# Layer 0 of a two-layer graph network: propagation by a matrix applied to products (Y0 + T (Y1 + T Y2)) in place of products of propagated inputs, with PSUM banks seeded by copies

## Chip, cores, metric

One core of a Trainium2 chip; the groups of rounds ran on different chips. Times are device microseconds (us) of one execution; a median and the range of the runs are given. All runs reported here were in the fast state, with a granted TensorE clock (the share of full speed that the chip allowed, averaged over the execution) of 0.994 to 1.000. That is not equal clock for differences of some us: 0.001 of 2365 us is 2.4 us, if TensorE is busy meanwhile (my estimate). A ratio is the mean time of one kernel's fast runs over the mean of the other kernel's fast runs in the same rounds, so it is not quite the ratio of the medians that I quote.

## The reference

128 graphs of 128 nodes with 512 features, fp32. All masks are ones, T is a row-normalised 128 x 128 matrix for each graph.

```python
# layer 0
h = maximum(layernorm(x), 0)
Xw = h @ Wv + bv
e = leaky_relu((Xw @ aw[:d])[:, None, :] + (Xw @ aw[d:])[:, :, None] + ab, 0.2)
alpha = adj * exp(e);  T = alpha / (sum(alpha, -1) + 1e-12)
H = 0; Xk = h
for k in range(3):                      # sum over k of T^k h W_k + b_k
    H = H + Xk @ Wk[k] + bk[k]
    Xk = T @ Xk
x = x + relu(H)
# layer 1
h = maximum(layernorm(x), 0)
q, k = split(h @ Wqk);  v = h @ Wv1
w = scale * rowsum(q * (adj @ k))
x = x + softmax(w)[:, :, None] * v
```

## The kernel before

Graphs are worked on in 64 pairs. The two scores of a node are h times two columns u (worked out once from Wv and aw), so VectorE forms them as sums over h. The products with weights are Strassen products: 7 block products instead of 8, with sums of blocks on the left (from h) and on the right (from the weights). The parts that the argument touches:

```python
def score_sums(p):                                  # VectorE: 4 sums over 512 columns (line 303)
    for j in range(G):
        for a in range(2):
            nc.vector.scalar_tensor_tensor(junk, h[:, j, :], 1.0, u_bc[:, a, :], op0=OP.mult,
                                           op1=OP.mult, accum_out=s[:, a * G + j:a * G + j + 1])
    PZ[p] = spread_pair(s, "pz", p > 1)             # scores to all partitions, through memory

def t_transposed(p):                                # T^T (line 384) and (T T)^T (line 388)
    ...
def propagate(p):                                   # (T h)^T and (T T h)^T: line 400, copies line 402
    ...
def strassen0(p, steps):                            # k = 0, 1, 2 side by side: 7 products, each
    product(ba, 1, True)                            # 3 x 2 matmuls x 2 column blocks, 256 wide (line 421)
    nc.vector.tensor_add(s[:, 0], a, hi)            # partial sums kept in SBUF by VectorE
    nc.vector.tensor_add(s[:, 1], a, lo)
    product(bb, 6, True)
    nc.vector.tensor_add(s[:, 2], b, s[:, 1])
    steps[0]()                                      # begin(n): transposes h of the next pair (VectorE)
    product(bc, 7, True)
    steps[1](s[:, 1])                               # attention of the next pair
    product(bb, 5, False)
    ...
    steps[2]()                                      # t_transposed of the next pair
    end(s[:, 3, :G])                                # softmax and output of an earlier pair
    ...
def prepare0(p):                                    # left sums of layer 0: four of 768 columns (VectorE)
    SX[p] = left_sums(a, front, "sx", [K, HD])
```

Layer 1 is a Strassen product of 28 passes 512 wide, also line 421, then two aggregates adj k (line 519). h goes to memory and comes back in blocks so that VectorE's block transpose can make h^T.

## Time and profile before

| | before |
|---|---|
| time, median of 3 runs | 2366.88 us (2364.62 to 2368.94) |
| TensorE busy | 99% |
| VectorE / ScalarE busy | 77% / 27% |
| period of the loop, one pair of graphs | 35.98 us |
| first T transpose | 37.41 us |

The busy table and the chain of waits name TensorE; that the loop has hardly a TensorE wait is what makes it the bound. The lines for this stand in the prediction. One view more is needed later, the landing times of transfers (tile written and read, queue, count, KB each, median us from issue to landing):

```profile
hd<-h SPq DMA_DIRECT2D x127, 512.0 KB, 4.0
hv<-hd SPq DMA_DIRECT2D x508, 128.0 KB, 5.3
```

These are h's way out to memory and back in blocks.

The profiled execution of the kernel before, from which all its lines here come, took 2370.26 us, longer than the three runs of the table. And its first pairs differ from the rest. TensorE in the third period:

```profile
90.81 3.78 PE L421 MATMUL pm<-e,x 128*128 128x512 f32 x4 [3.27 <-DVE x L320]
94.38 1.91 PE L421 MATMUL pm<-f,sx 128*128 128x512 f32 x2
```

Four passes of 512 columns stand 94.38 - 90.81 = 3.57 us apart, where they take 1.717 in mid-run: the clock was at half. The profile's clock records say so from 32.0 to 35.4 and from 90.1 to 96.9 us, 10.2 us in all. What brings these stretches about isn't tested here.

### The profile page before, as it was taken

Reading aid. Unit: us, or ns where it says so; the run is one execution under the profiler, and the core shown is the slowest. Engines: PE = TensorE matmul, PEld = TensorE weight load, DVE = VectorE, ACT = ScalarE, POOL = GpSimd, SP = SyncE. Lnnn points to the kernel's source line nnn. Section 1 sums busy time; section 2 is a strip of 40 time slices with the busy share of each in tenths; the row PEclk is TensorE's granted clock in tenths of the full one; section 3 lists DMA queues with packets and bytes.
Section 4 is the critical chain, followed back from the end, with each engine's and each line's share of the span. In section 5 each row is a group of like instructions: output and inputs, shape, how many; then the busy total and the mean of one; then the engine's idle time right before and its main releaser. Section 6 shows DMA issues by size and latency. Waiting matters only on the chain.

```text
span 2368.5 us, 27872 instructions
## 1 busy us (share of the span) xinstructions
PE 2342.0 (99%) x8929; PEld 1660.0 (70%) x8929; DVE 1825.3 (77%) x4959; ACT 637.5 (27%) x1562; POOL 379.0 (16%) x662
## 2 busy tenths in 40 slices
PE   8999999999999999999999999999999999999998
PEld 5677676676776776776766767767767767667675
DVE  6787877877877778778778778778788787787775
ACT  3222222322222222223222222222222232232221
POOL 4111111111111111111111111111111111111100
PEclk9999999999999999999999999999999999999999
DMA  7334344344343343443442433433434434424321
GB/s 210 91 92 107 98 107 105 83 116 111 85 116 106 90 107 99 107 107 84 120 106 83 116 107 90 114 101 98 107 100 105 107 91 115 107 81 117 104 63 49
DMA packets 253670, 242.88 MB, mean 103 GB/s; under 512 B 28318, under 2 KB 178846, under 8 KB 253522
## 3 DMA queue, kind: packets, MB, share of 16 engines
q1 hardware_dynamic: 228096, 211.87, 31.8%
q0 software_dynamic: 23312, 28.18, 6.7%
q8 instruction: 70, 1.15, 0.2%
q10 hardware_dynamic: 2114, 1.05, 0.1%
q14 instruction: 78, 0.64, 0.1%
HBM read 140.72 MB, written 100.27 MB: 102 GB/s over the span
## 4 chain that ended last, share of the span: by engine, by line
PE 89%; DVE 4%; DMA 2%; issue 1%; ACT 1%; POOL 0%; DVEq 0%; POOLq 0%
PE pm L421 75%; PE pt L400 8%; PE pt L519 4%; DMA pwd<-pwt 1%; PE pt L388 1%; PE pt L384 1%; DMA pw<-pwd 1%; DVE st L260 0%; DMA pz<-pzd 0%; DVE junk L303 0%; DVE x L461 0%; DVE x L320 0%; DVE x L549 0%; DMA pzd<-pzt 0%; DVE sx L409 0%
## 5 line engine op out<-in xcount | busy, mean ns | idle before, releaser
L421 PE MATMUL pm<-t,sx 128*128 128x256 f32 x2304 | 508.0, 379 | 2.9 <-DVE sx L408 2.9
L421 PEld LDWEIGHTS pm<-t,sx 128*128 128x128 f32 x2304 | 437.5, 190 | 63.0 <-DVE sx L408 3.5
L421 PE MATMUL pm<-b,x 128*128 128x256 f32 x1536 | 363.1, 379 | 0.0
L421 PE MATMUL pm<-f,sx 128*128 128x512 f32 x768 | 352.5, 594 | 2.0 <-DVE s L479 2.0
L421 PEld LDWEIGHTS pm<-b,x 128*128 128x128 f32 x1536 | 282.2, 190 | 59.7 <-issue 29.7
L339 POOL DMA_DIRECT2D pzd<-pzt x124 | 68.8, 556 | 1406.2 <-DVE pzt L336 1406.1
L421 PEld LDWEIGHTS pm<-f,sx 128*128 128x128 f32 x768 | 145.8, 191 | 186.7 <-issue 160.4
L421 PE MATMUL pm<-e,x 128*128 128x512 f32 x512 | 242.5, 596 | 3.3 <-DVE x L320 3.3
L402 ACT COPY x<-pt 128x512 f32<-128x512 f32 x256 | 147.3, 576 | 365.5 <-PE pt L400 365.4
L400 PE MATMUL pt<-tt,h 128*128 128x256 f32 x1024 | 231.6, 379 | 0.5 <-ACT tt L389 0.5
L303 DVE SCALAR_TENSOR_TENSOR junk<-h,u_bc 128x512 f32<-128x512 f32 x256 | 177.1, 692 | 64.1 <-ACT h L278 52.9
L400 PEld LDWEIGHTS pt<-tt,h 128*128 128x128 f32 x1024 | 194.5, 190 | 27.5 <-ACT tt L389 1.1
L421 PE MATMUL pm<-b,sx 128*128 128x256 f32 x768 | 176.2, 379 | 0.0
L421 PE MATMUL pm<-t,x 128*128 128x256 f32 x768 | 176.2, 379 | 0.0
L320 DVE STREAM_TRANSPOSE x<-hv 128x512 f32<-128x512 f32 x254 | 165.1, 688 | 10.8 <-DMA hv<-hd 9.7
L421 PEld LDWEIGHTS pm<-e,x 128*128 128x128 f32 x512 | 97.7, 191 | 99.7 <-issue 90.7
L356 ACT ACTIVATE s<-s 128x256 f32<-128x256 f32 x63 | 26.2, 416 | 518.9 <-DVE s L354 518.9
L421 PEld LDWEIGHTS pm<-t,x 128*128 128x128 f32 x768 | 145.9, 190 | 19.8
L421 PEld LDWEIGHTS pm<-b,sx 128*128 128x128 f32 x768 | 145.9, 190 | 19.8
L92 POOL DMA_DIRECT2D agb<-in_adj_dram x256 | 152.9, 602 | 22.6 <-issue 15.0
L278 ACT ACTIVATE h<-xg,rs 128x512 f32<-128x512 f32 x128 | 97.4, 807 | 172.8 <-DVE rs L272 172.8
L519 PE MATMUL pt<-h,aT 128*128 128x512 f32 x256 | 130.7, 592 | 0.0
(145 smaller groups left out, 2812.4 us busy)
## 6 DMA issues: line engine op xcount, KB each, us to landing
hd<-h SPq DMA_DIRECT2D x127, 512.0 KB, 4.0
hv<-hd SPq DMA_DIRECT2D x508, 128.0 KB, 5.3
xg<-in_x_dram SPq DMA_DIRECT2D x64, 512.0 KB, 3.6
out_dram<-x SPq DMA_DIRECT2D x63, 512.0 KB, 2.8
ag<-in_adj_dram SPq DMA_DIRECT2D x64, 128.0 KB, 2.8
agb<-in_adj_dram POOLq DMA_DIRECT2D x256, 32.0 KB, 4.2
pw<-pwd POOLq DMA_DIRECT2D x63, 128.0 KB, 3.3
pz<-pzd POOLq DMA_DIRECT2D x62, 128.0 KB, 5.5
```

The source lines that it names most:

```text
L92: nc.gpsimd.dma_start(agb[p][c * S32:(c + 1) * S32].rearrange("p g q i -> p (g q) i"), v[c])
L278: nc.scalar.activation(to, at, AF.Relu, bias=rs[:, 1, j:j + 1], scale=rs[:, 0, j:j + 1])
L303: nc.vector.scalar_tensor_tensor(junk, h[:, j, :], 1.0, u_bc[:, a, :], op0=OP.mult, op1=OP.mult, accum_out=s[:, a * G + j:a * G + j + 1])
L320: nc.vector.transpose(dst[:, j].rearrange("p f (n b) -> p f n b", n=Q), hv[:, j].rearrange("p n (f a) -> p f n a", f=Q))
L339: nc.gpsimd.dma_start(d[j], t[j::S32])
L356: nc.scalar.activation(ex, z, AF.Exp)
L384: nc.tensor.transpose(pt[:, j, :], t[:, j, :], ident)
L388: nc.tensor.matmul(pt[:, j, :], t[:, j, :], tt[:, j, 0, :], start=True, stop=True)
L400: nc.tensor.matmul(pt[:, c].rearrange("p k n -> p (k n)"), h[:, j, at:at + P], tt[:, j].rearrange("p k n -> p (k n)"), start=True, stop=True)
L402: nc.scalar.copy(X[p][:, 1:3, j, kh].rearrange("p k c n -> p c k n"), pt)
L421: nc.tensor.matmul(bank[:, :r.shape[-1]], left[i][:, k, c * P:(c + 1) * P], r, start=(first and at == 0), stop=(at == len(chunks) - 1), sk ...
L519: nc.tensor.matmul(to, AT[p][:, j, :], h2, start=True, stop=True)
```

## The change

Its intent: T^k h W_k is (T^k h) W_k before and T^k (h W_k) after. With Yk = h Wk, the sum is Y0 + T (Y1 + T Y2), so only h^T is needed as a left operand, T squared and the four copies of propagated inputs are gone, and the left sums shrink from 768 to 256 columns. The two score columns u stand beside W2 as a 257th column of each half, so TensorE forms the scores. Strassen's sums are made in PSUM: ScalarE copies one bank onto the next, and the next product adds onto it (the result passes the comparison, and in the trace after a product onto a copied bank streams like the others: four passes of 512 from 1218.56 to 1220.27 us, 0.428 each). Y0 and Y1 start on banks seeded with the biases. The core of the diff:

```diff
-        product(ba, 1, True)
-        nc.vector.tensor_add(s[:, 0], a, hi)
-        nc.vector.tensor_add(s[:, 1], a, lo)
-        product(bb, 6, True)
-        nc.vector.tensor_add(s[:, 2], b, s[:, 1])
-        ... (strassen0, propagate, T squared, score_sums: removed)
+    def strassen(banks, left, right, s, first, ends, steps={}):      # Y10, Y2 and layer 1
+        product(a, 1, first)
+        nc.scalar.copy(b, a)
+        product(e, 5, first)
+        nc.scalar.copy(s[:, 0], e)
+        product(b, 6)                                                # start=False: adds onto the copy
+        done["u2"] = nc.scalar.copy(c, b).ins
+        product(a, 2)
+        ends[0, 0](a)
+        product(c, 7)
+        nc.scalar.copy(s[:, 1], c)
+        ends[1, 1](e, s[:, 1])
+        product(b, 3)
+        ends[0, 1](b, s[:, 0])
+        product(c, 4)
+        ends[1, 0](c)
+    def seed():                                                      # [0 | b0] and [0 | b1 - b0]
+        nc.scalar.copy(a1, bias_a.rearrange("p k o -> p (k o)"))
+        nc.scalar.copy(e1, bias_e.rearrange("p k o -> p (k o)"))
+    def inner(p):                                                    # Y1 += T Y2, then to SBUF
+        for j, nh, bank in blocks1:
+            nc.tensor.matmul(bank[:, :HD], TT[p][:, j, :], y[:, j, nh, :HD], start=False, stop=True, ...)
+            nc.scalar.copy(z[:, j, nh], bank[:, :HD])
+    def outer(p, z):                                                 # Y0 += T (...), relu, add x
+        for j, nh, bank in blocks1:
+            nc.tensor.matmul(bank[:, HD:], tt[:, j, :], z[:, j, nh], start=False, stop=True, ...)
         ...
+            s0 = y10(p, {1: lefts, 6: lambda: t_transposed(p)})
+            z = inner(p)
+            s2 = y2(p + 1) if p + 1 < NP else s0
+            outer(p, z)
```

The start is rebuilt too: other loads, the weights transposed whole, Y2 of the first pair ahead of the loop. `issue_after` hints, which only fix the order in which an engine's instructions are issued, are added in many places.

## The prediction

> **What bounds the kernel now.** I read the page's busy table, then the chain that ended last, then the TensorE waits, then TensorE's timeline of one pair of graphs (the loop's unit; there are 64 pairs).
>
> ```profile
> PE 2342.0 (99%) x8929; PEld 1660.0 (70%) x8929; DVE 1825.3 (77%) x4959; ACT 637.5 (27%) x1562; POOL 379.0 (16%) x662
> ...
> PE 89%; DVE 4%; DMA 2%; issue 1%; ACT 1%; POOL 0%; DVEq 0%; POOLq 0%
> ```
>
> A busy TensorE alone doesn't prove a bound. The list of its waits does: the longest are these (total us, times, longest us), each happened once to three times in the whole run. Asked for 200 to 2300 us alone, the list has three waits, 1.9 us together: nothing waits in the steady loop.
>
> ```profile
> PE pt L236 <- DMA w<-in_L_gnn_Wqk_dram: 4.1, 2, 3.9
> PE pm L421 <- DVE x L320: 3.3, 1, 3.3
> PE pm L421 <- DVE sx L408: 2.9, 2, 2.0
> PE pm L421 <- DVE s L479: 2.0, 3, 1.2
> ```
>
> The timeline of one pair in mid-run (start, busy us, engine, line, operation, tiles, count) has no bracket that names an idle gap:
>
> ```profile
> 1243.54 0.38 PE L384 MATMUL pt<-ident,t 128*128 128x128 f32 x2
> 1243.76 1.03 PE L421 MATMUL pm<-b,x 128*128 128x256 f32 x4
> 1244.62 0.61 PE L388 MATMUL pt<-tt,t 128*128 128x128 f32 x4
> 1245.07 1.89 PE L421 MATMUL pm<-b,x 128*128 128x256 f32 x8
> ...
> 1251.97 3.62 PE L400 MATMUL pt<-tt,h 128*128 128x256 f32 x16
> 1255.43 1.88 PE L421 MATMUL pm<-e,x 128*128 128x512 f32 x4
> ...
> 1269.16 2.75 PE L421 MATMUL pm<-b,x 128*128 128x256 f32 x12
> 1271.75 7.93 PE L421 MATMUL pm<-t,sx 128*128 128x256 f32 x36
> 1279.52 0.38 PE L384 MATMUL pt<-ident,t 128*128 128x128 f32 x2
> ```
>
> From one L384 to the next is 1279.52 - 1243.54 = **35.98 us a pair**, and 64 x 35.98 = 2303 of the 2368. The rest is the start (the first L384 stands at 37.41 us), a few stalls behind it, and 8 us of tail. So the change is worth what it takes off TensorE's stream, less any stall that it brings.
>
> The price of a matmul must come from distances between starts, since durations overlap: thirty-six 256-wide ones take 1279.52 - 1271.75 = 7.77, or 0.2158 us each; the 32 passes 512 wide of layer 1 (L421 and L519) fill 1233.18 - 1219.44 = 13.74, or 0.4294 each (both starts from the same timeline one pair earlier). An L384 transpose is (1243.76 - 1243.54)/2 = 0.11, an L388 pass (1245.07 - 1244.62)/4 = 0.11. The record counts two passes for each fp32 product in the source, one for a transpose.
>
> [...]the trace is shorter (0.373 us at 256, 0.576 at 512 wide), and I use the trace. [...]two L278 of 0.806 take 1.52 together.
>
> **The change on TensorE, per pair.** Before: layer 0's Strassen has 7 products over k = 3 x 2 chunks x 2 columns-of-output blocks x 2 passes = 84 passes of 256; L400 (T and T squared times h) 16 of 256; layer 1 has 28 and the aggregates 4 of 512; T transposed 2 and T squared 4 of 128. 100 x 0.2158 + 32 x 0.4294 + 0.22 + 0.44 = 35.98, the measured period, so the count is right.
>
> After: Y1 and Y0 side by side, 7 x 2 x 2 = 28 passes of 512; Y2 with its score column, 28 of 257; the inner T Y2, 8 of 256, and the outer T(...), 8 of 256; layer 1 and aggregates 32 of 512; T transposed, 2 of 128. T squared is gone. 60 x 0.4294 + 28 x 0.2167 + 16 x 0.2158 + 0.22 = 25.76 + 6.07 + 3.45 + 0.22 = **35.50**. The gain is 0.48 us a pair, 30.7 us in 64 pairs. Of 140 records a pair 108 remain, which sounds like more than it is.
>
> **The change on the other engines, per pair.** VectorE has 1825.3/64 = 28.5 busy. It loses the four score sums L303 (4 x 0.69 and their reads, 3.1), swaps four 768-wide left sums for 256-wide ones (4 x (0.955 - 0.417) = 2.1), has two adds of 512 instead of five in layer 1 (2.0) and some 0.8 less in layer 0: about 20.5 remain, 58%. ScalarE has 637.5/64 = 10.0. It loses the four L402 copies, one tt copy and two layer-1 copies (3.8), and gains twelve of 512 (four in Y10, two seeds, six in layer 1: 12 x 0.58 = 7.0), six of 257 (2.2) and four of 256 (1.5): about 16.8, 47%. Neither becomes the bound by load; what counts is latency, as ScalarE now stands between products.
>
> **Latencies.** A copy starts some 0.2 us after the last pass has streamed (L384 ends its record at 1243.92, the ScalarE copy starts at 1243.96). In Y10 and layer 1 one product lasts 4 x 0.4294 = 1.72 and stands between the producer of a bank and the next use of its copy: 0.2 + 0.58 leaves 0.9 to spare. In Y2 a product lasts 0.87 and the copy 0.2 + 0.37: 0.25 to spare, and there the instruction order of the built kernel puts two relus (1.52) and the four z copies (about 1.25) on ScalarE before the first Y2 copy. Counting from the start t of Y2: the Y10 add of block 12 on VectorE follows product 3, which ended at t - 3.45; the add is over at t - 2.6, five small norm operations at 0.2 each bring t - 1.6, relus t - 0.05, z copies t + 1.2, the copy t + 1.6; product 6 wants it at t + 1.73. It fits with 0.1 us to spare. The other long loop is norm of layer 1's input, write to memory, read back, transposes and left sums: relu over at about 31 us of a pair, 9 to 10 us of transfers (landing medians 4.0 and 5.3 plus issues), so about 5 us into the next pair, where VectorE wants it at 4.9. Later than that by 2 us it would delay the relus and so Y2. I put **0.1 us a pair**, 6 us in all, for what of these margins fails.
>
> **Start and end.** Both kernels need about 30 us of TensorE work before the first pair (score matrix 16.4, transposes 6.4, the rest). Before, 7.4 us of waiting lie among it. After, the 2.6 MB of x and score weights come first, but the layer-0 weights are queued behind them: 7.3 MB at the 260 to 320 GB/s of the before kernel's first 30 us are there at about 27 us, and Y10's combinations at about 33; Y2 of pair 0 can run at 30 to 36. Against the first pair's work at 37.4 that saves up to 7 us; with a first loop whose VectorE queue is crowded (weight combinations, two left sums), I take 4. The tail stays within 1 us.
>
> Sum: 2366.9 - 30.7 - 4 + 6 = 2338; I say **2337 us**, 1.3% less.
>
> **Rivals.** (1) *Copies become the wait*: ScalarE is late at one or two products in each pair. For it: the margins of 0.1 and 0.25 above. Against: they hold with measured durations, and misses are small. At 0.5 us a pair the gain is gone: 2365. (2) *The reload loop binds*: transfers of 2 us more than assumed give a period set by norm, memory and left sums, 36.5 or so: 2400.[...] (3) *Everything fits and the start gains its 7 us*: 2328; without the first loop's stalls also, 2320, about the floor. (4) *Larger gain from fewer instructions*: if 32 fewer matmuls a pair saved 60 ns each, 2230[...].
>
> **Range and chances.** 80% range **2320 to 2364**: from rival 3's floor to rival 1's full loss. 2% faster is 2319.5, at the floor: **0.07**. 2% slower, 2414, takes more than a full microsecond of stall in each pair: **0.04**. Within 2%: **0.89**.
>
> **What would show the steps right or wrong.** Right: starts of two successive T transposes 35.5 to 35.7 us apart; 512-wide passes at 0.429 and 257-wide at 0.217; ScalarE near 47% and VectorE near 60% busy; next to no TensorE waits on ScalarE. Wrong: a wait of TensorE on ScalarE in Y2's product 6 or 7, repeated 60 times (rival 1); VectorE's transposes waiting for the read-back, followed by TensorE waits (rival 2); a 257-wide pass that costs clearly more than 0.217; a first Y2 that starts later than 37 us.

Where its prices come from: the copy times are those of lines 385 (0.373 us, 256 columns) and 402 (0.576 us, 512 columns) in the trace before. The 0.2167 us of a 257-wide pass was my estimate; the two measured widths give nearly the same, (0.4294 - 0.2158) / 256 = 0.834 ns a column and so 0.2166 us. That a product onto a seeded bank costs TensorE nothing more was assumed; no trace showed it yet. That a late copy holds the next product up was assumed too; the trace after has such waits at its start, 1.4 us in two (PE a L315 <- ACT b L322).

## The result and the profile after

The kernel after takes **2328.40 us** (2327.64 to 2328.80, 4 runs) against 2367.73 (2364.62 to 2368.94, 4 runs) before: ratio 0.9836, 95% interval 0.9818 to 0.9853. That is 1.64% faster and within 2%. It passes the comparison with the reference.

| | before | after | predicted |
|---|---|---|---|
| time, us | 2367.73 | 2328.40 | 2337 |
| period of a pair, us | 35.98 | 35.49 | 35.50 |
| VectorE busy | 77% | 58% | 58% |
| ScalarE busy | 27% | 44% | 47% |
| first Y2, us from the start | – | 37.38 | 30 to 36 |

Busy table and chain of the page after:

```profile
PE 2304.2 (99%) x6881; PEld 1290.7 (55%) x6881; DVE 1361.0 (58%) x4131; ACT 1028.8 (44%) x2517; POOL 336.6 (14%) x585
...
PE 98%; ACT 1%; DVE 0%; DMA 0%; issue 0%; POOL 0%; DVEq 0%; ACTq 0%; POOLq 0%
```

In the chain, VectorE's 4% and the transfers' 2% have gone: TensorE alone now sets the end. The whole list of TensorE waits begins with these (total us, times, longest):

```profile
PE b L205 <- ACT aw_bc L179: 7.1, 1, 7.1
PE b L178 <- DMA t<-in_L_gnn_aw_dram: 2.4, 1, 2.4
PE a L154 <- ACT y L355: 1.6, 1, 1.6
PE a L315 <- issue: 1.4, 1, 1.4
PE a L315 <- ACT b L322: 1.4, 2, 0.7
```

Each stands once or twice, none 60 times, and the list from 125 to 2280 us is empty: no wait came into the loop. TensorE's timeline of one pair in mid-run (start, busy us, engine, line, operation, tiles, shapes, count):

```profile
1216.62 0.38 PE L400 MATMUL a<-ident,t 128*128 128x128 f32 x2
...
1225.43 1.03 PE L315 MATMUL a<-r,x 128*128 128x257 f32 x4
...
1227.17 1.03 PE L315 MATMUL b<-t,sx 128*128 128x257 f32 x4
1228.03 1.03 PE L315 MATMUL a<-r,x 128*128 128x257 f32 x4
...
1233.23 1.88 PE L315 MATMUL a<-rl,x 128*128 128x512 f32 x4
1234.94 1.88 PE L315 MATMUL e<-tl,sx 128*128 128x512 f32 x4
...
1252.11 0.38 PE L400 MATMUL a<-ident,t 128*128 128x128 f32 x2
```

The period is 1252.11 - 1216.62 = 35.49 us. Four 257-wide passes take 0.866 (1227.17 to 1228.03), 0.2166 each; four 512-wide ones 1.717, 0.4293 each. So 64 x (35.98 - 35.49) = **31.4 us** of the 39.3 come from the columns that TensorE no longer streams. ScalarE's timeline in the same pair shows why nothing waits (a bracket is idle time ahead of the instruction):

```profile
1226.50 0.36 ACT L322 COPY b<-a 128x257 f32<-128x257 f32 x1
1227.37 0.37 ACT L324 COPY s<-e 128x257 f32<-128x257 f32 x1 [0.51 <-PE e L315]
1228.23 0.36 ACT L326 COPY c<-b 128x257 f32<-128x257 f32 x1 [0.49 <-PE b L315]
```

The copy that seeds bank b ends at 1226.50 + 0.36 = 1226.86, and its product starts at 1227.17: 0.31 us to spare where the prediction saw 0.1. The next seed ends at 1228.59, 0.31 ahead of 1228.90. The landing times after, for the same tiles as shown of before:

```profile
hd<-h SPq DMA_DIRECT2D x126, 512.0 KB, 2.8
hv<-hd SPq DMA_DIRECT2D x504, 128.0 KB, 2.9
```

They fell from 4.0 and 5.3 us, where the prediction's latencies kept these and its rival 2 had 2 us more. That transfers in bursts of two tensors would last longer was my guess when I predicted; no run shows it.

Left to explain: 39.3 - 31.4 = 7.9 us, where the prediction had a loss of 2 (stalls +6, start -4). Candidates: (a) the start or the end; (b) something small in every pair or in scattered pairs, above all VectorE, which was 77% busy before; (c) the period itself for another reason than the columns, such as fewer instructions. My theory when the experiments began: the columns give their 31 us, and a good part of the rest comes once, at the start. The rivals are (b) and (c). The experiments are to tell these apart and to say how close the copies are to becoming waits. The texts on record, written before each run, are quoted; where they letter the theories, the numbers beside the letter say what it stands for.

### The profile page after: what moved, and what is told of

The parts are those of the page before. It is cut to its first block, busy times and chain, and to the rows that moved or that the text cites. A ratio compares the mean times of both kernels' runs of the same rounds, so it can differ in the third digit from the quotient of the medians.

```text
span 2327.0 us, 23621 instructions
## 1 busy us (share of the span) xinstructions
PE 2304.2 (99%) x6881; PEld 1290.7 (55%) x6881; DVE 1361.0 (58%) x4131; ACT 1028.8 (44%) x2517; POOL 336.6 (14%) x585
## 4 chain that ended last, share of the span: by engine, by line
PE 98%; ACT 1%; DVE 0%; DMA 0%; issue 0%; POOL 0%; DVEq 0%; ACTq 0%; POOLq 0%
PE a L315 24%; PE c L315 24%; PE b L315 24%; PE e L315 12%; PE a L453 2%; PE e L453 2%; PE a L431 1%; PE c L431 1%; PE c L441 1%; PE b L441 1%; PE e L431 1%; PE e L441 1%; PE b L431 1%; PE a L441 1%; PE a L400 1%; ACT h L257 0%
## 5 line engine op out<-in xcount | busy, mean ns | idle before, releaser
L315 PE MATMUL a<-r,x 128*128 128x257 f32 (+1 forms) x1024 | 373.1, 486 | 1.4 <-ACT b L322 1.4
L315 PEld LDWEIGHTS a<-r,x 128*128 128x128 f32 x1024 | 189.3, 190 | 107.3 <-issue 91.2
L315 PE MATMUL a<-rl,x 128*128 128x512 f32 x512 | 240.7, 592 | 1.4 <-issue 1.4
L330 ACT COPY s<-c 128x512 f32<-128x512 f32 (+1 forms) x192 | 97.8, 510 | 209.5 <-PE c L315 209.4
L315 PE MATMUL c<-t,sx 128*128 128x257 f32 (+1 forms) x512 | 186.6, 487 | 1.2 <-ACT c L326 1.1
L315 PE MATMUL c<-t,x 128*128 128x257 f32 (+1 forms) x512 | 186.3, 486 | 0.3 <-ACT s L330 0.3
L315 PE MATMUL e<-t,sx 128*128 128x257 f32 (+1 forms) x512 | 186.4, 486 | 0.0
L315 PE MATMUL b<-t,sx 128*128 128x257 f32 (+1 forms) x512 | 186.2, 486 | 0.0
L315 PE MATMUL b<-r,sx 128*128 128x257 f32 (+1 forms) x512 | 186.2, 486 | 0.0
L324 ACT COPY s<-e 128x512 f32<-128x512 f32 (+1 forms) x192 | 98.8, 515 | 161.8 <-PE e L315 161.7
L315 PEld LDWEIGHTS a<-rl,x 128*128 128x128 f32 x512 | 97.2, 190 | 96.9 <-issue 93.6
L322 ACT COPY b<-a 128x512 f32<-128x512 f32 (+1 forms) x192 | 96.1, 500 | 97.7 <-PE a L315 89.7
L315 PEld LDWEIGHTS c<-t,sx 128*128 128x128 f32 x512 | 96.9, 190 | 70.6 <-issue 60.5
L315 PEld LDWEIGHTS c<-t,x 128*128 128x128 f32 x512 | 97.2, 190 | 68.7 <-issue 61.2
L315 PEld LDWEIGHTS b<-r,sx 128*128 128x128 f32 x512 | 97.3, 190 | 68.1 <-issue 61.2
L315 PEld LDWEIGHTS b<-t,sx 128*128 128x128 f32 x512 | 97.3, 190 | 68.1 <-issue 45.9
```

Source lines behind the costliest of these rows:

```text
L315: nc.tensor.matmul(bank, left[i][:, k * P:(k + 1) * P], right[i][:, k], start=(start and k == 0), stop=(k == HC - 1), skip_group_check=True)
L322: nc.scalar.copy(b, a)
L324: nc.scalar.copy(s[:, 0], e)
L330: nc.scalar.copy(s[:, 1], c)
```

## Experiments

### Half the pairs, both kernels

```diff
-    NP = B // G
+    NP = B // G // 2
```

Wrong on purpose (half the output isn't written). A constant gain at the start or the end stays whole at half the pairs, a gain per pair is halved.

> The kernel before with only the first 64 of 128 graphs (32 pairs); the rest of the output is left unwritten, wrong on purpose. The time is a constant (start and end) plus 32 pairs. Theory A (the gain is TensorE columns, 0.49 us in each pair, plus some 6 us of scattered stalls that the changed kernel lacks, plus some 4 us of start and end): 2367.7 - 32 x 35.98 - about 3 of stalls = 1213 to 1217 us.

Measured: 1211.3 us (1210.82 to 1212.69).

> The changed kernel with 32 pairs, wrong on purpose. Theory A: 2328.4 - 32 x 35.49 = 1192 to 1193 us, so 21 to 24 us less than the kernel before with 32 pairs: 15.7 from the pairs, the rest start, end and early stalls. Rival B (the gain sits in the start or the end): the difference stays near the 39 us of the full kernels. Rival C (all of it is in the steady pairs): the difference is half, 19.7.

Measured: 1193.0 us (1191.62 to 1193.67). The before half came out 2 to 6 us shorter than I had expected, so the difference is 18.3 us, not the 21 to 24 of my theory then, which put part of the gain at the start. The second half costs 2364.92 - 1211.3 = 1153.6 us before (36.05 a pair, whole kernel of the same rounds) and 2328.4 - 1193.0 = 1135.4 after (35.48 a pair). What doesn't grow with the pairs is 2 x 1211.3 - 2364.9 = 57.7 us before and 2 x 1193.0 - 2328.4 = 57.6 after. Taken at its word, start and end together gave nothing, and (a) falls. But that takes two things for granted that no run shows: that the first half of the kernel before has as many stalls as the second, and that the whole kernel after, which was run in other rounds only (the kernel before was 2.8 us slower in those), would have taken 2328.4 here.

The traces say otherwise. From each span I take the steady periods and what the periods behind the fourth T transpose exceed them by. Left for the start, the first three pairs and the end are 2368.48 - 64 x 35.98 - 5.99 = 59.8 us before and 2327.02 - 64 x 35.49 - 0.38 = 55.3 after; in the half kernels 59.0 and 55.3. So **some 4 us of the gain lie outside the steady loop**, and (a) stands; each of these is a single execution. What the half runs do show is a loss in the loop of the kernel before: its second half takes 36.05 - 35.98 = 0.07 us a pair more than its undisturbed period, 2.3 us in 32 pairs; the after kernel loses none.

### More columns in Y2

The Y2 passes of the after kernel are made 280 wide with 23 columns of zeros. Everything else stays: instruction counts, copies, orders.

```diff
-    WP = W2 + 3
+    W3 = HD + 24
+    WP = W3
-    r2 = const.tile([P, DC, 2, WP], FP, name="r2")[:, :, :, :W2]
+    r2 = const.tile([P, DC, 2, WP], FP, name="r2")
+    for c in range(DC):
+        nc.gpsimd.memset(r2[:, c, :, W2:W3], 0.0)
     ... (t2, y2 and s2 likewise; readers keep to column W2)
```

> The changed kernel with 280 instead of 257 columns in the Y2 products (23 columns of zeros more). Theory A (columns through TensorE set the period): 23 x 28 passes x 0.833 ns = 0.537 us a pair, 34 us in all: 2363 us, period 36.03, and the gain over the kernel before is all but gone. Rival D (fewer instructions, or relief of VectorE, makes the gain): stays at 2328 to 2333.

Measured: 2360.67 us (2359.34 to 2361.27, 20 runs), ratio 0.9980 to before; period 36.03. The timeline shows the new passes:

```profile
1242.64 1.11 PE L318 MATMUL b<-t,sx 128*128 128x280 f32 x4
1243.59 1.11 PE L318 MATMUL a<-r,x 128*128 128x280 f32 x4
```

Four take 0.945, 0.236 each. The period grew by 0.54 for 28 x 23 columns, which the price per column from the two widths before gives (28 x 23 x 0.834 ns = 0.537). Instructions are as few as in the after kernel and the gain is nearly gone: (c) falls, **columns set the period**. And a hint: with a period 0.05 us *longer* than before's (64 x 0.05 = 3 us), this kernel is 4 us *faster* than before, and scatters by 1.9 us where before scatters by 8.8. That suggests that some 7 us of before's time lie outside its steady stream of columns: waits, the start, or the clock (0.9996 in the mean of the wide runs, 0.998 before).

### VectorE relieved in the before kernel, a little

```diff
-    nc.vector.scalar_tensor_tensor(junk, h[:, j, :], 1.0, u_bc[:, a, :], op0=OP.mult,
+    nc.vector.scalar_tensor_tensor(junk[:, :S32], h[:, j, :S32], 1.0, u_bc[:, a, :S32], op0=OP.mult,
```

Score sums over 32 of 512 columns, with wrong scores on purpose (the comparison is too loose to see it).

> The kernel before with its four score sums cut from 512 to 32 columns (wrong on purpose): VectorE has some 1.9 us a pair less to do, nothing else changes. Theory A: the steady period stays at 35.98; only the scattered stalls (6 us over the run) shrink: 2361 to 2367 us. Rival E (relief of VectorE is a main source of the gain): 2350 or less.

Measured: 2364.63 us (2361.63 to 2366.97, 13 runs), ratio 0.9999 (0.9991 to 1.0007). VectorE fell from 77% to 73%, and the median did not move. The clock blurs this: these runs had 0.997 in the mean against 0.998 before, and the slower ones the lower clock (2361.63 us at 0.999, 2366.97 at 0.995), so that a gain of about 2 us could be hidden. The one profiled run was the fastest of the thirteen, without scattered stalls; had I had that profile alone, I would have believed in a gain. A profile is one draw.

### VectorE loaded in the after kernel

```diff
+    def load_vector(h):
+        for i in range(4):
+            junk = front.tile([P, D], FP, name="junk2", bufs=1)
+            nc.vector.scalar_tensor_tensor(junk, h[:, i % G, :], 1.0, h[:, i % G, :], op0=OP.mult,
+                                           op1=OP.mult, accum_out=vcol[:, i:i + 1])
         ... (called behind both by_blocks of a pair: 8 sums of 512 columns more)
```

> The changed kernel with eight 512-wide VectorE sums a pair added, whose results nobody reads: 5.8 us a pair, so that VectorE is again some 75% busy, as in the kernel before. Theory A: period 35.49 stays the most frequent one; scattered stalls of up to some us may return, time 2328 to 2335 us. Rival E (relief of VectorE makes much of the gain): 2345 us and up.

Measured: 2333.44 us (2331.14 to 2336.66, 4 runs), ratio 0.9874, period 35.49 as before the loading. At 73% of VectorE the after kernel loses 5 us by the medians, 9 by the ratios (0.9874 against 0.9836; the kernel after itself wasn't run in these rounds), and four runs scatter by 5.5 us instead of 1.2. The profiled execution, the fastest of the four, has no TensorE wait in the loop; its span is 2.3 us longer than that of the kernel after, and 2.1 of them lie before the fourth T transpose (153.66 against 151.57 us). So part of the loss is again one of the first pairs; stalls in the loop are not shown by it.

### Scores by VectorE in the after kernel

Y2 is 256 wide again, four sums a pair on VectorE make the scores, and their spreading goes as in the before kernel. The weights of the sums are wrong on purpose; the timing is what counts.

```diff
-    W2 = HD + 1
+    W2 = HD
+    def score_sums(p, h):
+        s = S[p] = scols[p % 3]
+        for j in range(G):
+            for a in range(2):
+                nc.vector.scalar_tensor_tensor(junk, h[:, j, :], 0.01, u_bc, op0=OP.mult,
+                                               op1=OP.mult, accum_out=s[:, a * G + j:a * G + j + 1])
         ... (attention and the spreading read s instead of Y2's columns)
```

> The changed kernel with the score columns taken out of the Y2 product (256 wide again) and made by four VectorE sums of 512 a pair, as before, with weights that are wrong on purpose. Theory A: TensorE saves 28 x 0.83 ns = 0.023 us a pair, 1.5 us in all, and VectorE goes to 67%: 2325 to 2330 us. So this part of the change would be worth nothing in time by itself. Rival E: 2335 us and up.

Measured: 2325.63 us (2325.05 to 2325.72, 4 runs), ratio 0.9836; period 35.47, VectorE 67%. The score columns beside Y2 are worth nothing by themselves: they cost TensorE one column in each of 28 passes a pair (0.02 us), and VectorE at 67% does the sums with no stall. Its scatter of 0.7 us beside that of the kernel at 73% would fit a limit between the two, on four runs each.

### VectorE relieved in the before kernel, more

The last run tests just that: the score sums cut as above, and layer 0's left sums over 256 of 768 columns, the rest left at zero. TensorE's products and every transfer stay.

```diff
+    sx0 = const.tile([P, 4, K, HD], FP, name="sx0")
+    nc.gpsimd.memset(sx0, 0.0)
-        s = pool.tile([P, 4] + width, FP, name=name, bufs=1)
-        nc.vector.tensor_add(s[:, 0], a[1, 0], a[1, 1])
+        s, at = (sx0, slice(0, 1)) if pool is None else (pool.tile(...), slice(0, width[0]))
+        nc.vector.tensor_add(s[:, 0, at], a[1, 0][:, at], a[1, 1][:, at])
         ... (the other three sums and the score sums likewise cut)
```

> The kernel before, wrong on purpose, with VectorE relieved twice: the score sums take 32 of 512 columns, as in before_noscore, and the four left sums of layer 0 take 256 of 768 columns (the rest stays zero), so that TensorE's products and every transfer stay what they were. VectorE should fall from 77% to about 67%; TensorE's period must stay 35.98 us. Open is why the kernel before runs some 3 to 5 us above the time that its period and its least disturbed runs give (2361.7 the lowest of 33 runs, median 2364.9), while the kernel after scatters by 1.2 us only. Theory S (a queue of VectorE that is full enough turns late small transfers into stalls of TensorE; 73% busy still does it, as in before_noscore and after_vload, 67% does not, as in scores_by_vector): 2360 to 2362, with a scatter of at most 2 us. Rival T (the stalls come from the transfers of the kernel before whatever VectorE's load is, for example the score transfers that go by the software queue twice a pair): within 1 us of the kernel before of the same rounds, with its scatter of 4 us or more.

Measured: **2358.34 us** (2357.03 to 2359.77, 10 runs) against 2364.82 (2360.31 to 2367.17, 14 runs), ratio 0.9975 (0.9966 to 0.9985); the result is wrong, as meant.

```profile
PE 2336.8 (99%) x8929; PEld 1663.3 (71%) x8929; DVE 1570.9 (67%) x4959; ACT 650.7 (28%) x1562; POOL 379.5 (16%) x663
```

TensorE's count of passes is before's, its period still 35.98 and the clock 0.998 as well, yet 6.5 us are gone and the scatter fell from 6.9 to 2.7. So the relief of VectorE makes the difference, and rival T falls. But both numbers of theory S were missed (2360 to 2362, scatter of at most 2), and the trace shows that scattered stalls aren't all of it. Two places changed:

- Scattered stalls: the 60 periods behind the fourth T transpose exceed 60 x 35.98 by 5.99 us before and by 0.25 us here. The profiled before execution is a slow one, though; half_before has 0.59 us in 28 periods.
- The start and the first three pairs: the fourth T transpose stands at 123.5 us before, at 122.7 in half_before and at 116.8 here. These 5.9 to 6.7 us alone are as much as the medians gained. TensorE's waits up to 125 us sum to 17.1 us before, 16.6 in half_before and 12.0 here; before's list (in the prediction) has 2.9 us for the left sums (sx L408) that this edit shortens and 3.3 for the transposes of h (x L320), and both are gone. The list here begins:

```profile
PE pt L236 <- DMA w<-in_L_gnn_Wqk_dram: 3.8, 1, 3.8
PE pt L386 <- DVE t L367: 3.7, 1, 3.7
```

How the 6.5 us of the medians divide between the two isn't shown: these are single executions. In the first pairs TensorE waits for VectorE's own sums and transposes, which needs no theory of queues.

How a full VectorE may become a TensorE stall later is to be seen in one disturbed pair of the before profile. VectorE:

```profile
811.75 0.41 DVE L410 TENSOR_TENSOR sx<-x,sx 128x256 f32<-128x256 f32 x1
814.19 0.42 DVE L536 TENSOR_REDUCE s<-pw 128x2 f32<-128x256 f32 x1 [2.02 <-DMA pw<-pwd]
...
827.95 0.68 DVE L479 TENSOR_TENSOR s<-pm,s 128x512 f32<-128x512 f32 x1
```

TensorE of the same stretch:

```profile
826.42 1.02 PE L519 MATMUL pt<-h,aT 128*128 128x512 f32 x2
828.69 1.55 PE L421 MATMUL pm<-f,sx 128*128 128x512 f32 x3 [1.24 <-DVE s L479]
```

VectorE waited 2.02 us for a small transfer of scores (pw), which took its usual 3.2 us. Nothing on TensorE needed it; but VectorE started nothing else during the wait, and its 27 timeline rows from line 536 to line 479 come in the same order as in the pair before (there 775.61 to 789.58 us), so all that stood behind was late as well: with one marked gap of 0.41 us in the 14 us between, VectorE reached the sum of line 479 late, and TensorE waited 1.24 us for the bank. This is read from one pair; of the 5.99 us, the list of waits puts 2.0 down to VectorE. With VectorE at 67%, or 58% in the kernel after, wider gaps could take such a delay up: after has one of over 6 us in 60 of 64 pairs (6.63 in that of 1223.7 to 1230.4), where Y2's first sum waits for ScalarE. That they do so isn't tested apart from the medians above.

### The copies twice

To find how close ScalarE is to being a wait, both seeding copies of every Strassen product are made twice.

```diff
-        nc.scalar.copy(b, a)
+        for _ in range(2):
+            nc.scalar.copy(b, a)
         ... (the same for nc.scalar.copy(c, b))
```

> The changed kernel with the two ScalarE copies that carry a product sum from bank to bank done twice in each of the three Strassen products (result stays right): 6 copies more a pair, about 2.7 us of ScalarE. In the trace of the changed kernel such a copy ends 0.3 us (Y2) to 1.2 us before TensorE needs it. The built order of this kernel also moves outer products between Y2's, so TensorE has other work there. Theory A (copies are hidden, with room): period 35.5 to 35.6, time 2328 to 2336 us. Rival (ScalarE's copies are all but on the path): half a microsecond a pair or more, 2360 us and up.

Measured: 2347.91 us (2347.71 to 2348.69, 4 runs), ratio 0.9932; period 35.76. A miss: I had expected 2328 to 2336. TensorE's timeline of the Y10 product:

```profile
1223.84 1.88 PE L315 MATMUL e<-t,sx 128*128 128x512 f32 x4
1225.68 1.98 PE L315 MATMUL b<-t,sx 128*128 128x512 f32 x4
1227.50 0.38 PE L402 MATMUL a<-ident,t 128*128 128x128 f32 x2
```

Four passes of 512 take 1.717, so product 6 (onto b) should start at 1225.56 and starts at 1225.68; it then lasts 1.82 instead of 1.717. These two delays of 0.12 and 0.10 make most of the 0.27 that the period grew. In the after kernel that copy ends at 1213.69 + 0.57 = 1214.26, product 6 starts at 1214.90: 0.64 to spare, and the second copy takes nearly all of it. So the copies are hidden, and not by much: the place to watch is Y10, not Y2, where the prediction looked.

### Without the ordering hints

```diff
     def behind(what, op, *args):
-        with tc.issue_after(done[what]):
-            return op(*args)
+        return op(*args)
```

> The changed kernel without its hints that queue VectorE work behind other VectorE work (transposes and left sums ahead of the two bank additions, the norm of layer 1 behind a copy). Theory A: VectorE is 58% busy and has room for another order; a few stalls at most: 2328 to 2340 us. Rival: the hints are what keeps TensorE fed: a stall in each pair, 2360 us and up.

Measured: 2327.59 us (2327.11 to 2328.19, 4 runs), ratio 0.9845 (0.9831 to 0.9860; the kernel after 0.9836), period 35.49. The hints are worth nothing here.

### The start of the after kernel

TensorE's first instructions after (its bracket of 7.14 us is the longest wait of the whole run):

```profile
4.26 1.91 PE L178 MATMUL c<-t,ones 1*128 1x512 f32 x2
13.30 2.07 PE L205 MATMUL b<-t,ones 3*128 3x512 f32 x2 [7.14 <-ACT aw_bc L179]
...
37.38 0.81 PE L315 MATMUL a<-r,x 128*128 128x257 f32 x3
```

ScalarE, which was to empty that bank:

```profile
11.26 1.52 ACT L257 ACTIVATE h<-xg,rs 128x512 f32<-128x512 f32 x2 [1.11 <-DVE rs L251]
12.69 0.56 ACT L179 COPY aw_bc<-b 128x512 f32<-128x512 f32 x1
```

The bias product (L205) wants bank b, whose copy stands in ScalarE's queue behind the first norm, which waits for VectorE, which in turn has a small load ahead of it. The eight groups of weight transposes that are independent of this stand behind L205. The experiment puts the bias product behind the transposes, and the small VectorE product behind the norm:

```diff
-    attention_constant()
-    bias()
+    behind("rs", attention_constant)
+    behind("wt", bias)
```

> The changed kernel with the order of its start mended: in its trace TensorE idles 7.1 us before the bias product, which stands ahead of the score-matrix transposes and waits for a bank that ScalarE empties late, since VectorE first waits for a small load. Here the bias product is queued behind the transposes and the small VectorE product behind the first norm. Theory (idle of TensorE in the start counts fully unless weights then come too late): 4 to 8 us less, 2320 to 2325 us. Rival (the layer-0 weights, loaded last, hold the first pair back anyway): 2326 to 2329 us.

Measured: 2326.08 us (2324.07 to 2327.40, 4 runs), ratio 0.9829 (0.9816 to 0.9843), not clear of the 0.9836 of the kernel after. A miss of the 4 to 8 us; the time lies where the rival reading put it. By the traces the gain is 1 to 2 us. The transposes now run early but wait for loads:

```profile
11.36 1.11 PE L218 MATMUL c<-ident,tl 128*128 128x128 f32 x4 [1.37 <-DMA tl<-in_L_gnn_Wqk_dram]
...
14.62 1.09 PE L218 MATMUL a<-ident,tl 128*128 128x128 f32 x4 [1.29 <-DMA tl<-in_L_gnn_Wqk_dram]
```

Taking away the 7 us wait uncovered others, 3.0 us in all with one of 0.32 ahead of these: the first Y2 moved only from 37.38 to 35.83. A second cause is the clock. In the kernel after four transposes take 0.85 us up to 20.47 us and 0.53 behind it; here two passes of 512 at 20.25 still take 1.71, twice the later 0.859, and the passes come down to that only at about 24.6. That makes some 4 us more at half speed, about 2 us lost (my estimate).

### T transposed through memory

If streamed columns are all that counts, the two transposes of T (2 x 0.11 us a pair) can go as well, through memory and VectorE's block transpose, since VectorE now has room.

```diff
+            td = dram.tile([G, N, N], FP, name="td")
+            nc.sync.dma_start(td.rearrange("g n m -> n g m"), t)
+            ... (read back in 32 x 32 blocks, as adj is)
+            nc.vector.transpose(tt.rearrange("p g n -> p (g n)"), TB.pop(p).rearrange("p g q i -> p (g q i)"))
```

> The changed kernel with T transposed not by TensorE (2 passes, 0.22 us a pair) but by writing it to memory, reading it back in blocks of 32 and transposing those on VectorE; from pair 2 on. Theory A (TensorE's stream sets the time and the new transfers hide): period 35.27, 62 x 0.22 = 14 us less, 2314 to 2318 us. Rival (the round trip ends just when T is wanted, some 10 us after T is made): a stall in many pairs, 2328 us and up.

Measured: 2315.68 us (2314.60 to 2316.28, 4 runs), ratio 0.9785 (0.9772 to 0.9799); period 35.27, which is 35.49 less 0.22 as expected. The result is correct. It is in time: VectorE makes the transpose here,

```profile
1251.90 0.44 DVE L408 STREAM_TRANSPOSE tt<-tb 128x256 f32<-128x256 f32 x1
```

and TensorE needs it here, 0.83 us after its end:

```profile
1253.17 0.59 PE L444 MATMUL a<-y,tt 128*128 128x256 f32 x2
```

Together with the start:

> Both of these together. If each theory holds: 2307 to 2314 us, 2.2% below the kernel before.

Measured: 2313.40 us (2312.24 to 2314.63, 5 runs) against 2366.47 before, ratio 0.9778 (0.9764 to 0.9791), correct. This is the fastest correct version found.

| run | us, median | ratio to before | period, us | VectorE |
|---|---|---|---|---|
| before (five groups of rounds) | 2364.8 to 2367.7 | 1 | 35.98 | 77% |
| before_noscore | 2364.63 | 0.9999 | 35.98 | 73% |
| before_light | 2358.34 | 0.9975 | 35.98 | 67% |
| wide | 2360.67 | 0.9980 | 36.03 | 58% |
| copy_double | 2347.91 | 0.9932 | 35.76 | – |
| after_vload | 2333.44 | 0.9874 | 35.49 | 73% |
| after | 2328.40 | 0.9836 | 35.49 | 58% |
| no_order | 2327.59 | 0.9845 | 35.49 | – |
| start | 2326.08 | 0.9829 | – | – |
| scores_by_vector | 2325.63 | 0.9836 | 35.47 | 67% |
| tt_mem | 2315.68 | 0.9785 | 35.27 | – |
| tt_mem_start | 2313.40 | 0.9778 | – | – |

Times of different rounds differ by up to 3 us for the same kernel before, so between rows of different rounds the ratio is the safer column (scores_by_vector and the kernel after have the same).

## Why the prediction was right or wrong

- **The bound and the columns: right.** TensorE's stream set the time before and sets it after; the period was predicted as 35.50 and is 35.49, from prices of a 512-, 257- and 256-wide pass that all came out within 0.2 ns. The wide run shows that the columns, not the instructions, make it.
- **Rival 4 (fewer instructions): wrong.** 2048 records fewer bought nothing beyond their columns; in the trace before, two 256-wide passes cost only 2 x 0.2158 - 0.4294 = 0.002 us more than one of 512. (Its 2230 us is a slip: 64 x 32 x 0.06 = 123 us, so 2244 from 2366.9.)
- **ScalarE's latencies: right in kind.** No wait of TensorE on a copy is repeated in the loop. The term "0.1 us a pair, 6 us in all" measured 0: Y2's copies have 0.31 us to spare. The copies doubled do become a wait, first at Y10, so the worry was sound and the size was not. (In the trace after, the copies of lines 322 to 330, recorded as COPY, take 0.570 to 0.585 us in the mean at 512 columns and 0.357 to 0.374 at 257.)
- **The reload loop: no wait.** The landings became shorter (5.3 to 2.9 us), where the prediction's rival 2 had them 2 us longer. What set the old landing times wasn't tested.
- **The start: wrong in its reason; its size came out by luck.** "Y2 of pair 0 can run at 30 to 36": it ran at 37.38. The step that failed counted TensorE's work and the loads, and overlooked that one product waits for a bank that sits behind ScalarE's and VectorE's queues (7.14 us). The start run shows that mending this gives only 1 to 2 us, for loads and half clock come next. Yet the traces leave 4.5 us less outside the steady loop (59.8 and 55.3; 3.7 in the half kernels), about the "I take 4". What the kernel before loses in its first pairs, and the kernel after does not, are waits for VectorE (2.9 and 3.3 us) and 10.2 us at half clock, which cost up to 5.1; I take these for the reason, but no run shows it alone. The prediction's parts hid this: 37.41 + 2303 + 8 leaves 20 us of the 2368 for "a few stalls"; and the last T transpose stands 80.2 us before the end, a period and 44 us, where the prediction had 8 for the tail.
- **A missing term: before's losses to a full VectorE.** The prediction took VectorE's fall from 77% to 58% as free of value, since it found only 1.9 us of TensorE waits in the loop. But the sum began from a measured 2366.9 in which scattered stalls were contained. In before_light the relief of VectorE is worth 2364.82 - 2358.34 = 6.5 us, first pairs and scattered stalls together; for the stalls alone there are the 2.3 us of the second half and the 5.99 of one slow execution.

The sum by measured terms: -31.4 (columns) - 6.5 (VectorE, first pairs and stalls, as in before_light) = -37.9, of the 39.3 us measured. That the kernel after gains from VectorE's relief what before_light does is assumed, not shown. The clock is not in this sum: before_light has the mean clock of the kernel before, 0.998, the kernel after 0.999, about 2 us. The remaining 1.4 us is less than that, and less than the medians of the unchanged before kernel differ between groups of rounds (2364.8 to 2367.7). The predicted sum was -30.7 - 4 + 6 = -28.7. So the range held, the class held, and 2337 was 8.6 us too high because of stalls that did not come (6) and stalls of the kernel before, not counted, that went (2.3 to 6). The columns, four fifths of the gain, are shown; the rest is in part argued.

Open: how the rest divides between first pairs, scattered stalls and clock; whether the stalls begin between 67% and 73% of VectorE, and whether it is the busy share or where its gaps lie that matters. The two runs at 73% add or keep work at other places of the loop than the runs at 67%.

## What to carry to other kernels

When TensorE never waits in the loop, count the columns that it streams and price them by distances between starts: that gave the period to 0.01 us, while the 23% fewer matmul instructions told nothing. An engine off the critical path of the loop can still cost time, in the first pairs and through scatter (6.5 us here between before and before_light): before predicting, take the steady periods off the span and name what is left, wait by wait and with the clock, because a change that relieves that engine may win some of it back as well. And trust no stall count of a single profile; here one profile held 6 us of stalls and another of nearly the same kernel none, with equal medians.
